# Laying dt and dt u in memory for one read per chunk, and placing the stages of four layers by their scans

## The chip, the cores and the metric

The kernel runs on one core of a Trainium2 chip. The metric is the time of the program on the device in microseconds; the runs before the change give 5587.08 us as the median of three (5577.02 to 5589.37). A separate, profiled execution took 5573.59 us, of which the profile's span is 5571.9 us. The text uses the profile's names of the engines: PE multiplies matrices (PEld loads its weights), DVE, ACT and POOL work element by element, and SP issues the transfers between memory and the on-chip buffer.

## The reference

Thirty-two sequences of 256 tokens with 256 features go through four layers, in fp32. Each adds its result to its input x:

- layer 0, a Mamba layer: normalize x, modulate, permute the tokens, scan, permute back, gate;
- layer 1, softmax attention with 16 heads, with a normalized and modulated output;
- layer 2, a Mamba layer without the permutation;
- layer 3, linear attention with 16 heads.

A Mamba layer projects the normalized input to a scan input and a gate of 512 channels each, runs a convolution of four taps and a SiLU over the first (this is u), and projects u to a step size dt per channel and to vectors B and C of 16 states per token. The core is

```
dA  = exp(dt_t[:, :, None] * A)                      # A is negative, 512 x 16
hst = hst * dA + (dt_t * u_t)[:, :, None] * B_t[:, None, :]
y   = einsum('bds,bs->bd', hst, C_t)                 # for t = 0 .. 255
```

followed by y + u D, a product with silu(z) and the output projection. The recurrence over 256 tokens runs for 512 x 16 = 8192 pairs of channel and state in each sequence and layer.

## The kernel before

**One scan.** `mamba_scan(L, b)` runs the recurrence of layer L (0 or 2) and sequence b in 16 steps k. A step handles one chunk of 128 channels (c = 0 to 3) and one group of four states (g = 0 to 3). The 128 partitions hold 32 channels (`CB`) for each of the four states of the group (`NG`), and the free dimension holds the four quarters of the chunk (`QB`) with 256 tokens each: 1024 elements. For that, dt and dt u of the chunk have to stand on the partitions four times, once for each state. A step consists of

- POOL: b = dt u times B (2.37 us each);
- ACT: h = exp(A dt), four operations of 256 columns;
- DVE: the scan h = h x + b over 1024 columns (2.29 us);
- the product with C: on DVE for even g (1.22 us), on POOL for odd g (2.36 us);
- PE: sums over the four states into y.

The tiles b lie in a ring of four buffers, h in two.

**What a scan needs first.** `mamba_ahead(L, b)` computes the scan's inputs: normalization, projection, convolution, u, B and C, dt (a softplus on ACT) and, on POOL, dtu = dt u. B and C go to memory and come back spread over partitions, eight fetches per scan. dt and dt u are written to memory (tiles `dtd` and `dtud`, 512 channels by 256 tokens, line 794), one transfer of 512 KB each. For each chunk, `mamba_scan` reads them back into `dtr` and `dtur`. As the state groups need four copies, and the quarters lie apart in memory, each tile takes four reads of 128 KB into 32 partitions each (line 839). `dtr` and `dtur` have two buffers each, so a chunk's reads wait until the chunk two before it has been used. All these transfers are issued on SP's queue, in order; a transfer that waits holds those behind it.

**Who sets the order.** The program isn't written in the order in which it runs. Each operation becomes a `Step` with an estimated cost and a due number, and `Plan.order` (line 255) replays the engines with these costs: at each time it takes, for an engine, the step with the earliest due number among those that could begin soonest. It also keeps track of buffers. The resulting order of each engine is fixed in the program, and the hardware then runs each engine's list in order. A fetch counts as 0.4 us of SP and 3 us until its data are there (`fetch`, `late`).

[...]the plan also tracks PE's work over windows. Where the work in the last window would fall under `NEED` = 1.1[...], and nothing else of weight is ready, `usual` (line 287) puts in a filler: a matmul with zeros into y, seen in the profile as y<-rows,zeros.

**Due numbers.** At the end of the function a loop over i from -1 to 34 places the stages in units of two: iteration i covers the due numbers 2i to 2i + 2. Layer 0's scan of sequence i stands in the first half. Layer 2's preparation for sequence i - 2 stands in the first half too, and its scan in the second. Layer 0's preparation for sequence i + 1 stands in the second half; attention of sequence i - 1 in 2i to 2i + 1.55; linear attention of sequence i - 3 from 2i + 1.55 to 2i + 2. So layer 2 follows two sequences behind layer 0. Below, a period is the pair of one first-layer scan (layer 0) and one second-layer scan (layer 2), a unit the time from the start of one scan to the start of the next.

Of the kernel before, what the change touches and what calls it, by code (L numbers as in the profile page):

```python
# [8 lines left out]
F32 = mybir.dt.float32  # L9
# [7 lines left out]
P = 128  # L17
S = 256
# [3 lines left out]
DI = 512  # L22
IC = DI // P
# [8 lines left out]
NG = 4  # L32
SG = NS // NG
CB = P // NG
QB = P // CB
# [28 lines left out]
}  # L64
NROWC = 512
MASK_ROW, MAX_ROW = DH, DH + 1


class Virtual:
# [72 lines left out]
class Step:  # L142


    def __init__(self, cost, due, then, area):
        self.cost, self.due, self.then, self.area = cost, due, then, area
        self.engine, self.calls, self.table = None, [], None
        self.before, self.after, self.new, self.uses = set(), [], [], set()
        self.parts, self.opens, self.closes = False, None, False


class Clock:
# [45 lines left out]
class Plan:  # L198
# [1 line left out]


    NEAR = 0.25
    NEED = 1.1
    IDLE = 0.47
    LATENCY = 0.15
    SWITCH = 1.3
# [30 lines left out]
    def use(self, s, view, written):  # L237
        t = view.tile
        keep = []
        for one in t.seen:  # L240
            o, lo, hi, w = one
            clash = o is not s and lo < view.hi and view.lo < hi and (w or written)
            if clash:
                s.before.add(o)
            if not (written and view.lo <= lo and hi <= view.hi and o is not s):
                keep.append(one)
        keep.append((s, view.lo, view.hi, written))
        t.seen = keep
        if t not in s.uses:
            s.uses.add(t)  # L250
            if not t.steps and t.real is None:
                s.new.append(t)
            t.steps.append(s)
# [169 lines left out]
def kernel(ctx: ExitStack, tc: tile.TileContext, t, out: bass.AP):  # L423
# [219 lines left out]
    def fetch(out, in_, late=3.0):  # L643
        at(0.4, then=late)
        nc.sync.dma_start(out=out, in_=in_)

    def mrow_of(b):

        m = mrow_bufs[mrow_at[0] % 2]
        mrow_at[0] += 1  # L650
        fetch(m[0:1, :], mterm[3][b : b + 1, :])
        return m
# [51 lines left out]
    def mamba_ahead(L, b, st):  # L704

        nm = f"{L}_{b}"
        x = x_of[b]
        gate = w2.tile([P, D], F32, name=f"gate_{nm}", tag="gate")
        fetch(gate, gate_d[L][b].partition_broadcast(P))

        xh = normed(x, nm)
        if L == 0:
            ps = mm(f"ga_{nm}")
            pv = ps.rearrange("p (c t) -> p c t", c=DC)
            for c in range(DC):
                at(0.96)
                for s in range(ST):
                    nc.tensor.matmul(pv[:, c, :], lhsT=xh[:, s, c * P : (c + 1) * P], rhs=onehot[:, s, :],
                                     start=(s == 0), stop=(s == ST - 1))
        else:  # L720
            pv = transposed(xh, nm)
        hT = w2.tile([P, DC, S], F32, name=f"hT_{nm}", tag="hT")
        evacuated(hT, pv, AF.Identity, lambda c: shift[L][:, c, b : b + 1], lambda c: gain[L][:, c, b : b + 1])

        yield 0.2

        wi = wt[f"L{L}_in"]
        xpad = w1.tile([P, IC, 3 + S], F32, name=f"xpad_{nm}", tag="tmp")
        at(0.3)
        nc.gpsimd.memset(xpad[:, :, 0:3], 0.0)  # L730
        sz = w2.tile([P, IC, S], F32, name=f"sz_{nm}", tag="sz")
        for m2 in range(IC):
            ps = mm(f"in_{nm}_{m2}")
            pv = ps.rearrange("p (c t) -> p c t", c=2)
            for j in range(2):
                m = 2 * m2 + j
                at(0.96)
                for k in range(DC):
                    nc.tensor.matmul(pv[:, j, :], lhsT=wi[:, k, m * P : (m + 1) * P], rhs=hT[:, k, :],
                                     start=(k == 0), stop=(k == DC - 1))  # L740
            at(0.49)
            if m2 < 2:
                nc.scalar.copy(xpad[:, 2 * m2 : 2 * m2 + 2, 3:], pv)
            else:
                nc.scalar.activation(sz[:, 2 * m2 - 4 : 2 * m2 - 2, :], pv, AF.Silu)
            yield 0.25 + 0.05 * m2

        u = w2.tile([P, IC, S], F32, name=f"u_{nm}", tag="u")
        for c2 in range(2):
            ps = mm(f"cv_{nm}_{c2}")  # L750
            for j in range(2):
                c = 2 * c2 + j
                at(1.83)
                for k in range(4):
                    nc.tensor.matmul(ps[:, j * S : (j + 1) * S], lhsT=taps[L][:, c, k, :],
                                     rhs=xpad[:, c, k : k + S], start=(k == 0), stop=(k == 3))
            at(0.8)
            for j in range(2):
                c = 2 * c2 + j
                nc.scalar.activation(u[:, c, :], ps[:, j * S : (j + 1) * S], AF.Silu, bias=col(f"L{L}_conv_b", c))  # L760
            yield 0.45 + 0.1 * c2


        ps = mm(f"xp_{nm}")
        R = DTR + 2 * NS
        at(1.9)
        for k in range(IC):
            nc.tensor.matmul(ps[:R, :S], lhsT=wt[f"L{L}_xp"][:, k, :], rhs=u[:, k, :],
                             start=(k == 0), stop=(k == IC - 1))
        xd = w2.tile([R, S], F32, name=f"xd_{nm}", tag="xd")  # L770
        at(0.28)
        nc.scalar.copy(xd, ps[:R, :S])
        bc_d = memory.tile([2 * NS, S], F32, name=f"bc_{nm}", tag="bc_d")
        fetch(bc_d, xd[DTR:R, :])

        yield 0.7


        dt = w1.tile([P, IC, S], F32, name=f"dt_{nm}", tag="tmp")
        dtu = w1.tile([P, IC, S], F32, name=f"dtu_{nm}", tag="dtu")  # L780
        for c2 in range(2):
            ps = mm(f"dt_{nm}_{c2}")
            at(1.06, area=512)
            for j in range(2):
                c = 2 * c2 + j
                nc.tensor.matmul(ps[:, j * S : (j + 1) * S], lhsT=wt[f"L{L}_dt"][:, 0, c * P : (c + 1) * P],
                                 rhs=xd[:DTR, :], start=True, stop=True)
            at(0.73)
            for j in range(2):
                c = 2 * c2 + j  # L790
                softplus(dt[:, c, :], ps[:, j * S : (j + 1) * S], col(f"L{L}_b_dt", c))
        yield 0.8

        dd = [memory.tile([DI, S], F32, name=f"{what}d_{nm}", tag=f"{what}d") for what in ("dt", "dtu")]
        at(2.4)
        nc.gpsimd.tensor_tensor(dtu, dt, u, ALU.mult)
        fetch(dd[1].rearrange("(c p) t -> p c t", p=P), dtu)
        at(0.3)
        nc.gpsimd.memset(dt[:, :, 0:1], NEVER)
        fetch(dd[0].rearrange("(c p) t -> p c t", p=P), dt)  # L800

        st[L, b] = (dd, u, sz, gate, bc_d)

# [10 lines left out]
    def mamba_scan(L, b, st):  # L814
# [16 lines left out]
        for k in range(IC * SG):  # L831
            yield k / steps
            c, g = divmod(k, SG)
            if g == 0:
                dr = []
                for i, what in enumerate(("dt", "dtu")):
                    dr.append(rep.tile(shape, F32, name=f"{what}r_{nm}_{c}", tag=what))
                    src = dd[i][c * P : (c + 1) * P, :].rearrange("(q d) t -> d q t", d=CB)
                    for n in range(NG):
                        fetch(dr[-1][n * CB : (n + 1) * CB], src)  # L840
            if c % 2 == 0 and g == 0:
                y = ybank.tile([P, 2, S], F32, name=f"y_{nm}_{c}", tag="y")
            b_ = ring.tile(shape, F32, name=f"b_{nm}_{k}", tag="b")
# [278 lines left out]
    def first_ahead(b, st):  # L1122
        x_of[b] = xp.tile([P, ST, D], F32, name=f"x_{b}", tag="x")
        fetch(x_of[b], t["x"][b].rearrange("(s p) d -> p s d", p=P))
        yield 0.05
        yield from mamba_ahead(0, b, st)

    def placed(gen, begin, end):

        place = begin  # L1130
        while True:
            yield place
            try:
                place = begin + (end - begin) * next(gen)
            except StopIteration:
                return
# [11 lines left out]

    x_of, ready = {}, {}
    for i in range(-1, B + 3):
        gens, i2 = [], 2.0 * i
        if 0 <= i < B:
            gens.append(placed(mamba_scan(0, i, ready), i2, i2 + 1.0))
        if 0 <= i - 2 < B:
            gens.append(placed(mamba_ahead(2, i - 2, ready), i2, i2 + 0.9))
            gens.append(placed(mamba_scan(2, i - 2, ready), i2 + 1.0, i2 + 2.0))
        if 0 <= i + 1 < B:
            gens.append(placed(first_ahead(i + 1, ready), i2 + 1.0, i2 + 1.9))  # L1160
        if 0 <= i - 1 < B:
            gens.append(placed(attention(i - 1), i2, i2 + 1.55))
        if 0 <= i - 3 < B:
            gens.append(placed(linear_attention(i - 3), i2 + (1.55 if i - 1 < B else 0.0), i2 + 2.0))
        interleave(gens)
    plan.carry_out()


# [90 lines left out]
```

## Time and profile before

| | |
|---|---|
| median of three runs | 5587.08 us |
| profiled execution, its own time | 5573.59 us |
| its span | 5571.9 us |
| granted PE clock, mean over the span | 0.958 |
| first b of the first scan | 119.64 us |
| first b of layer 2's scan of sequences 28, 29, 30, 31 | 5026.1, 5196.47, 5337.82, 5469.87 us |
| loads of ACT's function tables | 563 records, 1283 ns each |
| transfers on the hardware queue | 443.08 MB in 468480 packets, 30.3% of 16 engines' span |

The profile lists, for each group of instructions, the busy time, the mean duration of one, and the idle time of the engine just ahead of it with what ended it. A timeline lists single instructions with start and duration. A table of windows gives busy times in chosen stretches with the granted PE clock (1.00 is full, 0.50 half) and the mean busy share of the sixteen transfer engines. A matmul in fp32 has two records. The names are those of the tiles: b<-dtur,B is POOL's first product, h<-dtr,Aneg the exponential, b<-b,C POOL's product with C, s and ex the attention's scores and their exponentials.

### The profile page before, as it was taken

Reading aid. Unit: us, or ns where it says so; the run is one execution under the profiler, and the core shown is the slowest. Engines: PE = TensorE matmul, PEld = TensorE weight load, DVE = VectorE, ACT = ScalarE, POOL = GpSimd, SP = SyncE. Lnnn points to the kernel's source line nnn. Section 1 sums busy time; section 2 is a strip of 40 time slices with the busy share of each in tenths; the row PEclk is TensorE's granted clock in tenths of the full one; section 3 lists DMA queues with packets and bytes.
Section 4 is the critical chain, followed back from the end, with each engine's and each line's share of the span. In section 5 each row is a group of like instructions: output and inputs, shape, how many; then the busy total and the mean of one; then the engine's idle time right before and its main releaser. Section 6 shows DMA issues by size and latency. Waiting matters only on the chain.

```text
span 5571.9 us, 81780 instructions
## 1 busy us (share of the span) xinstructions
PE 5011.1 (90%) x29884; PEld 3375.8 (61%) x29884; DVE 4135.5 (74%) x4290; ACT 3638.7 (65%) x7325; POOL 3921.9 (70%) x2130
## 2 busy tenths in 40 slices
PE   6899898999999999999999999999999999998876
PEld 5566555566666566666566666566666566666554
DVE  2767787687777777777777787777787777777754
ACT  2567676676676666676666676676676676676543
POOL 1768777777777776777776677777677777677544
PEclk7999999999999999999999999999999999999988
DMA  4323223323223323323332323332323332323111
GB/s 141 84 58 93 78 77 91 84 70 87 81 75 92 85 78 78 88 69 92 85 78 77 89 70 95 81 84 76 84 73 91 86 87 72 87 77 79 50 48 50
DMA packets 468883, 448.30 MB, mean 80 GB/s; under 512 B 41600, under 2 KB 465120, under 8 KB 468480
## 3 DMA queue, kind: packets, MB, share of 16 engines
q1 hardware_dynamic: 468480, 443.08, 30.3%
q8 instruction: 235, 3.85, 0.3%
q14 instruction: 168, 1.38, 0.1%
HBM read 365.19 MB, written 77.73 MB: 79 GB/s over the span
## 4 chain that ended last, share of the span: by engine, by line
PE 21%; DVE 12%; POOL 10%; ACT 8%; DMA 6%; issue 4%; SPq 1%; POOLq 0%; ACTq 0%; DVEq 0%
POOL b L398 9%; ACT h L398 5%; PE cv L398 4%; DVE h L398 4%; PE y L398 4%; PE s L398 4%; DVE b L398 3%; PE in L398 3%; PE o L398 3%; DMA dtr<-dtd 2%; DMA dtd<-dt 2%; SPq L398 1%; ACT L398 1%; DVE st L398 1%; POOL dtu L398 1%
## 5 line engine op out<-in xcount | busy, mean ns | idle before, releaser
L398 POOL TENSOR_TENSOR b<-dtur,B 128x1024 f32<-128x1024 f32 x1024 | 2405.6, 2370 | 670.8 <-DMA dtur<-dtud 308.9
L398 ACT ACTIVATE h<-dtr,Aneg 128x256 f32<-128x256 f32 x4096 | 1699.0, 465 | 309.3 <-DVE b L398 182.5
L398 POOL TENSOR_TENSOR b<-b,C 128x1024 f32<-128x1024 f32 x512 | 1205.7, 2355 | 589.2 <-DVE b L398 564.0
L398 DVE TENSOR_TENSOR_SCAN h<-h,b 128x1024 f32<-128x1024 f32 x512 | 1173.0, 2291 | 510.4 <-ACT h L398 296.0
L398 DVE TENSOR_TENSOR_SCAN b<-h,b 128x1024 f32<-128x1024 f32 x512 | 1167.8, 2281 | 65.3 <-POOL b L398 34.8
L398 PE MATMUL y<-rows,zeros 128*128 128x256 f32 x3298 | 881.0, 399 | 0.0
L398 ACT ACT_TABLE_LOAD x563 | 722.3, 1283 | 171.4 <-DMA dtr<-dtd 116.0
L398 PE MATMUL y<-b,sel 128*32 128x256 f32 x8192 | 648.5, 395 | 176.8 <-POOL b L398 93.2
L398 PEld LDWEIGHTS y<-rows,zeros 128*128 128x128 f32 x3298 | 604.6, 195 | 193.9 <-issue 128.2
L398 DVE TENSOR_TENSOR b<-h,C 128x1024 f32<-128x1024 f32 x512 | 623.9, 1219 | 17.6 <-DVE h L398 0.5
L398 PE MATMUL in<-hT,w_L_in 128*128 128x256 f32 x2048 | 513.2, 390 | 14.8 <-DVE nm L398 5.0
L398 PE MATMUL cv<-xpad,taps 128*128 128x256 f32 x2048 | 499.1, 389 | 14.2 <-ACT xpad L398 9.2
L398 PEld LDWEIGHTS y<-b,sel 128*32 128x32 f32 x8192 | 177.8, 109 | 491.5 <-POOL b L398 181.1
L398 DVE TENSOR_REDUCE nm<-s 128x2 f32<-128x512 f32 x512 | 328.6, 683 | 178.2 <-PE s L398 176.3
L398 PEld LDWEIGHTS in<-hT,w_L_in 128*128 128x128 f32 x2048 | 370.8, 190 | 147.8 <-issue 36.8
L398 PEld LDWEIGHTS cv<-xpad,taps 128*128 128x128 f32 x2048 | 375.1, 190 | 125.3 <-issue 52.4
L398 ACT ACTIVATE ex<-s 128x512 f32<-128x512 f32 x512 | 276.2, 590 | 123.5 <-PE s L398 121.8
L398 PE MATMUL s<-q,k 32*128 32x256 f32 x2048 | 337.7, 412 | 18.2 <-ACT dt L398 12.2
L398 PE MATMUL s<-k,q 32*128 32x256 f32 x2048 | 300.0, 404 | 2.2 <-ACT sz L398 1.1
L398 PE MATMUL o<-w_L_out,u 128*128 128x256 f32 x1024 | 284.3, 433 | 7.7 <-ACT xpad L398 7.0
L398 ACT ACTIVATE xh<-x,nb,rs 128x256 f32<-128x256 f32 x256 | 138.6, 592 | 222.7 <-DVE nb L398 213.6
L398 PEld LDWEIGHTS s<-q,k 32*128 32x128 f32 x2048 | 200.6, 188 | 136.7 <-issue 75.3
(466 smaller groups left out, 5849.3 us busy)
## 6 DMA issues: line engine op xcount, KB each, us to landing
dtur<-dtud SPq DMA_DIRECT2D x1024, 128.0 KB
dtr<-dtd SPq DMA_DIRECT2D x1024, 128.0 KB
B<-bc SPq DMA_DIRECT2D x256, 128.0 KB
C<-bc SPq DMA_DIRECT2D x256, 128.0 KB
dtud<-dtu SPq DMA_DIRECT2D x64, 512.0 KB
dtd<-dt SPq DMA_DIRECT2D x64, 512.0 KB
x<-in_x SPq DMA_DIRECT2D x32, 256.0 KB
gate<-gate_d SPq DMA_DIRECT2D x64, 128.0 KB
```

The costliest lines, as they stand in the source:

```text
L398: made.append(getattr(engine, name)(*[real(a) for a in args], **{k: real(v) for k, v in kw.items()}))
```

## The change

1. *Layout.* `dtd` and `dtud` become tiles of shape [32, 4, 4, 256]: channel within a quarter, chunk, quarter, token. The four quarters of a chunk lie side by side in memory, 4 KB for each of 32 channels. A new function `by_channel` writes each of them in four transfers of 128 KB, one for each quarter, from 32 partitions each. The plan is told that the four don't clash (`group`, `aside`).
2. *Reads.* Each `dtr` and `dtur` tile takes one transfer of 512 KB into 128 partitions, whose source repeats the 32 channels four times. The plan counts 4 us for it.
3. *Places.* The due numbers now follow from a list of scans, with layer 2 one sequence behind layer 0 (`LAG` = 1): layer 0's scan of sequence 0, then of 1, layer 2's of 0, layer 0's of 2, layer 2's of 1, and so on, 64 scans without a gap. Every other stage is placed relative to the scans before and after it: attention of b begins with the end of layer 0's scan of b and takes 0.8 of the time to layer 2's preparation; that preparation starts 0.7 ahead of its scan and ends 0.2 ahead; linear attention begins after layer 2's scan and takes 1.2. All stages are interleaved at once and no longer by iteration.
4. *Fillers.* `NEED` becomes 1.05.

What each engine computes for the result stays the same.

```diff
-    NEED = 1.1
+    NEED = 1.05
...
-            clash = o is not s and lo < view.hi and view.lo < hi and (w or written)
+            aside = s.group is not None and o.group is s.group and w and written
+            clash = o is not s and lo < view.hi and view.lo < hi and (w or written) and not aside
...
+    def by_channel(d, src):
+        for q in range(QB):
+            at(0.4, then=3.0).group = d.tile
+            nc.sync.dma_start(out=d[:, :, q, :], in_=src[q * CB : (q + 1) * CB])
...
-        dd = [memory.tile([DI, S], F32, name=f"{what}d_{nm}", tag=f"{what}d") for what in ("dt", "dtu")]
+        dd = [memory.tile([CB, IC, QB, S], F32, name=f"{what}d_{nm}", tag=f"{what}d") for what in ("dt", "dtu")]
         at(2.4)
         nc.gpsimd.tensor_tensor(dtu, dt, u, ALU.mult)
-        fetch(dd[1].rearrange("(c p) t -> p c t", p=P), dtu)
+        by_channel(dd[1], dtu)
         at(0.3)
         nc.gpsimd.memset(dt[:, :, 0:1], NEVER)
-        fetch(dd[0].rearrange("(c p) t -> p c t", p=P), dt)
+        by_channel(dd[0], dt)
...
-                    dr.append(rep.tile(shape, F32, name=f"{what}r_{nm}_{c}", tag=what))
-                    src = dd[i][c * P : (c + 1) * P, :].rearrange("(q d) t -> d q t", d=CB)
-                    for n in range(NG):
-                        fetch(dr[-1][n * CB : (n + 1) * CB], src)
+                    dr.append(rep.tile([P, QB * S], F32, name=f"{what}r_{nm}_{c}", tag=what))
+                    fetch(dr[-1], dd[i][:, c, :, :].rearrange("d q t -> d (q t)").unsqueeze(0)
+                          .to_broadcast([NG, CB, QB * S]), late=4.0)
+                dr = [v.rearrange("p (q t) -> p q t", q=QB) for v in dr]
...
-    for i in range(-1, B + 3):
-        gens, i2 = [], 2.0 * i
-        if 0 <= i < B:
-            gens.append(placed(mamba_scan(0, i, ready), i2, i2 + 1.0))
...
+    scans = [(L, i - L // 2 * LAG) for i in range(B + LAG) for L in (0, 2) if 0 <= i - L // 2 * LAG < B]
+    place = {scan: n for n, scan in enumerate(scans)}
+    for b in range(B):
+        first, second = place[0, b], place[2, b]
+        gap = second - first - 1
+        gens.append(placed(first_ahead(b, ready), first - FIRST_AHEAD[0], first - FIRST_AHEAD[1]))
+        gens.append(placed(mamba_scan(0, b, ready), first, first + 1))
+        until = second - AHEAD[0] * min(1.0, gap / 2)
+        gens.append(placed(attention(b), first + 1, first + 1 + ATTN * (until - first - 1)))
+        gens.append(placed(mamba_ahead(2, b, ready), until, second - AHEAD[1] * min(1.0, gap / 2)))
+        gens.append(placed(mamba_scan(2, b, ready), second, second + 1))
+        gens.append(placed(linear_attention(b), second + 1, second + 1 + LINEAR))
+    interleave(gens)
```

with `LAG` = 1, `FIRST_AHEAD` = (1.4, 0.1), `AHEAD` = (0.7, 0.2), `ATTN` = 0.8 and `LINEAR` = 1.2.

More of the change, by code (lines that the diff above doesn't have):

```diff
@@ L66 @@
 MASK_ROW, MAX_ROW = DH, DH + 1
+LAG = 1
+FIRST_AHEAD = (1.4, 0.1)
+AHEAD = (0.7, 0.2)
+ATTN = 0.8
+LINEAR = 1.2
 class Virtual:
@@ L148, in __init__ @@
         self.before, self.after, self.new, self.uses = set(), [], [], set()
-        self.parts, self.opens, self.closes = False, None, False
+        self.parts, self.opens, self.closes, self.group = False, None, False, None
 class Clock:
@@ L241, in use @@
             o, lo, hi, w = one
-            clash = o is not s and lo < view.hi and view.lo < hi and (w or written)
+            aside = s.group is not None and o.group is s.group and w and written
+            clash = o is not s and lo < view.hi and view.lo < hi and (w or written) and not aside
             if clash:
                 s.before.add(o)
-            if not (written and view.lo <= lo and hi <= view.hi and o is not s):
+            if aside or not (written and view.lo <= lo and hi <= view.hi and o is not s):
                 keep.append(one)
@@ L1147, in interleave @@
                 live.remove(one)
-    x_of, ready = {}, {}
-    for i in range(-1, B + 3):
-        gens, i2 = [], 2.0 * i
-        if 0 <= i < B:
-            gens.append(placed(mamba_scan(0, i, ready), i2, i2 + 1.0))
[L1156 to L1165, printed above, removed]
+    x_of, ready, gens = {}, {}, []
+    scans = [(L, i - L // 2 * LAG) for i in range(B + LAG) for L in (0, 2) if 0 <= i - L // 2 * LAG < B]
[11 more added lines that the diff above has]
+    interleave(gens)
     plan.carry_out()
```

## The prediction

> **What bounds the kernel now.** I read the page first, for whether one engine is full.
>
> ```profile
> span 5571.9 us, 81780 instructions
> PE 5011.1 (90%) x29884; PEld 3375.8 (61%) x29884; DVE 4135.5 (74%) x4290; ACT 3638.7 (65%) x7325; POOL 3921.9 (70%) x2130
> L398 POOL TENSOR_TENSOR b<-dtur,B 128x1024 f32<-128x1024 f32 x1024 | 2405.6, 2370 | 670.8 <-DMA dtur<-dtud 308.9
> L398 PE MATMUL y<-rows,zeros 128*128 128x256 f32 x3298 | 881.0, 399 | 0.0
> ```
>
> PE looks full, but 881 us are filler matmuls (y<-rows,zeros). No engine is the bound over the whole span, so I cut it into stages by POOL's timeline: a scan starts with its first b. From 1440.62 to 5026.1 us the starts repeat every 164.7 us: 99 us for a first-layer scan, 66 for a second-layer scan. Busy times of these stages, then of the stretch from the first b to dtu, and of the stretch from dtu's end to the second scan's first b (columns: window, length, busy us of PE, PEld, DVE, ACT, POOL, granted clock, DMA share, GB/s):
>
> ```profile
> 1440.62:1539.62 99.00, 89.95 (x514) 63.01 (x513) 77.58 (x85) 62.73 (x123) 62.48 (x35) 0.97 0.28 75
> 1539.62:1605.31 65.69, 61.48 (x415) 39.25 (x414) 51.62 (x46) 51.14 (x106) 59.89 (x32) 1.00 0.36 94
> 1440.62:1518.62 78.00, 70.39 (x401) 49.84 (x399) 65.47 (x71) 52.79 (x107) 55.27 (x30) 0.96 0.17 49
> 1520.97:1539.62 18.65, 17.21 (x105) 11.49 (x104) 10.82 (x12) 7.61 (x12) 4.87 (x4) 1.00 0.76 182
> ```
>
> The second scan is POOL-bound (59.9 of 65.7). The first is not: POOL idles 22.7 us among the attention's PE and DVE work, then waits for the memory round trip of dt u. POOL's timeline at that place:
>
> ```profile
> 1518.62 2.35 POOL L398 TENSOR_TENSOR dtu<-dt,u 128x1024 f32<-128x1024 f32 x1
> 1529.46 2.35 POOL L398 TENSOR_TENSOR b<-b,C 128x1024 f32<-128x1024 f32 x1 [3.70 <-DVE b L398]
> 1539.62 9.31 POOL L398 TENSOR_TENSOR b<-dtur,B 128x1024 f32<-128x1024 f32 x4 [7.82 <-DMA dtur<-dtud]
> ```
>
> So a period is 78.0 + 2.35 + 18.65 + 65.7 = 164.7 us. PE worked 17.2 of the 18.65 us, mostly on real work, so this wait is only partly a loss today.
>
> How fast a transfer runs depends on its form. Around the first scan few things run, and four windows show one kind each: B and C broadcasts; the writes of dt and dt u; the broadcasts left over; the reads into dtr and dtur.
>
> ```profile
> 94.00:101.00 7.00, 5.78 (x25) 4.39 (x24) 0.00 (x0) 2.97 (x5) 2.45 (x2) 1.00 0.26 84
> 102.00:104.00 2.00, 0.00 (x0) 0.00 (x0) 0.00 (x0) 0.00 (x0) 0.00 (x0) 0.95 1.05 356
> 105.00:108.00 3.00, 0.00 (x0) 0.00 (x0) 0.00 (x0) 0.00 (x0) 0.00 (x0) 0.50 0.27 94
> 112.00:119.00 7.00, 7.00 (x30) 5.91 (x29) 0.00 (x0) 0.84 (x2) 0.00 (x0) 0.85 1.14 196
> ```
>
> The broadcasts never pass a share of about a quarter: four of sixteen engines, 94 GB/s. The present reads use all engines but get only 196 GB/s.
>
> [...]
>
> **The change, part by part.** Instruction orders are written out from both programs; durations are those of the rows.
>
> (1) *Reads.* Per chunk of 128 channels, eight reads of 128 KB become two of 512 KB. Their source is [4, 32, 1024] with a repeated first dimension, against 128 rows: B's form, hence four engines. Price of one: 5.6 us at 94 GB/s[...]. I take 5.2. Today a tile takes 2.7 us at 196 GB/s. If I am wrong and it spreads over sixteen, 1.4. In a steady period 16 tiles need 83 us and 16 B/C fetches of 128 KB 22 us of the same four engines, 105 of some 163: not the bound, but transfers queue up.
>
> (2) *Writes.* Two become eight, each reading 32 partitions: 5.5 us for both tiles at the reads' 196 GB/s instead of 3. A write landed 3.1 us after issue at 1521, and 8.4 us at 99.5, behind B and C. In the new order all eight B/C fetches stand directly ahead of it in SP's queue; I take 6.
>
> (3) *Round trip at the second scan.* dtur is read for two chunks, then dtr. From dtu's end: 6 + 5.2 + 2.6 for landing (the last scan's last read was issued at 5466.6 and its b began at 5469.9: 3.3 less 0.7 of transfer) = 13.8 us to the first b, and 6 + 3 x 5.2 + 2.6 = 24.2 to the first exponential (today 18.65 and about 19). POOL then has four b (9.4 us) before the ring of four buffers is full; the fifth needs exponential, scan, product and sum of the first, 1.7 + 2.3 + 1.2 + 0.6 after 24.2, so POOL waits 6.8 us more. On ACT's queue dt now stands behind the scan's last exponential, with xd's copy and a table load: 3 us ahead of dtu. Behind that exponential wait DVE's scans and PE's sums.
>
> (4) *Order of stages.* Attention moves mostly under the second scan. Per unit, counts times the rows' means: real PE work 86.0/54.1 becomes 79.2/60.8 us, DVE 69.4/47.3 becomes 62.7/54.0. Between first b and dtu POOL has 25 large operations instead of 22: 25 x 2.36 + 4 x 0.93 = 62.7 us; in the second unit 55.4. Its idle time amid other work is 22.7 + 5.8 = 28.5 us per period now; at best both units stand like the second one now, 12. With 7 us of PE and DVE work moved out of the full unit into the one with 35 fillers, I take 19.
>
> (5) *Fillers.* 50 per period become 41 (15/35 to 11/30), 0.53 us each (two records of 267 ns busy): 4.8 us of PE, of which the lower NEED explains part. Nothing separate is added: it lies within (4). In all 1649 become 1415.
>
> (6) *At nothing:* SP's issues fall from 2976 to 1824 at some 0.45 us; SP mostly waits for others, so nothing; were it the limit at the scan's start, fourteen fewer issues would gain 6 us there. Table loads 565 to 525 at 1.28 us lie under ACT's 35% idle; uncovered, 1.6 us per period.
>
> Sum of a steady period: 62.7 + 3 + 2.35 + 13.8 + 55.4 + 6.8 + 19 = 163 us.
>
> (7) *Ends.* Before: first b at 119.6, then 59 scans to 5026.1, then five scans in 546 us, because the last two sequences run through attention and the second layer's preparation uncovered (141 and 132 us, then 102). After: 120 + 74 for the first scan as now; the second lasts 145, because attention and preparation of sequence 0 stand uncovered behind it (10 us tail of the scan, 85 for attention, where the last one took 103 under a scan, 28 preparation from the 5417 to 5445 us of the last one, 15 round trip, rest normalizing); then 60 scans at half a period; scan 63 another 145 for the same reason; 103 for the last. 587 + 30 x 163 = 5477 us, 1.7 more outside the span (5573.6 against 5571.9), and the runs' median lies 13.5 above the profiled one: 5492 us, say 5490, 1.7% faster.
>
> **Rivals.**
> *Slower: the four-engine reads decide.* Place: the start of each second-layer scan. Break-even is a period of (5571.9 - 587) / 30 = 166.2 us, 3.2 more than my sum: first exponential at 27.5 instead of 24 us after dtu. For it: the queue on four engines at two thirds load, and a plan that allows 4 us for a read. Against: chunks later in a scan have some 14 us of POOL work as cover. With 6 us more per period, 169: 5670 us.
> *The reads spread over sixteen engines.* Round trip 10 and 13 us, no second wait: 62.7 + 3 + 2.35 + 10 + 55.4 + 19 = 152.5; 5177 us. Against: B's share of 0.27.
> *Only the ends change.* The better mix gives back just what the reads cost: 164.7, thus 587 + 4941 + 15 = 5543 us.
> *The clock.* NEED 1.05 leaves less margin[...]. The clock is 0.97 to 1.00 now.[...]
>
> **How the numbers follow.** Likeliest, a period of 155.5 to 165.5 (its own range 5270 to 5570, ends-only included): 0.50. Sixteen engines: 0.10. Within 0.2%, about what a measurement can tell, or 165.8 to 166.6: 0.05, the clock in it. Slower by the reads: 0.35. Faster 0.60, slower 0.35. The idle time in (4) reaches 28.5, a period of 172 and 5760 us; I leave out the last stretch and the lowest case: 5300 to 5710.
>
> **What would show it.** Right: a DMA share near 0.25 while dtur lands, first b about 14 and first exponential about 24 us after dtu, periods of 160 to 165 us, a gap of some 145 us before the third scan and the last. Wrong: dtur landing at a share near 1, or waits on dtr inside scans, or POOL still idle 28 us per period amid attention.

## The result and the profile after

The changed kernel takes 5947.48 us (median of four runs, 5935.32 to 5958.41) against 5582.05 us for the kernel before on the same chip: a ratio of 1.0653, with a 95% interval of 1.0624 to 1.0682. It is 6.5% slower, where 1.7% faster had been forecast. The page of its profile:

```profile
span 5938.0 us, 79158 instructions
...
PE 4985.7 (84%) x29416; PEld 3333.2 (56%) x29416; DVE 4093.0 (69%) x4290; ACT 3575.1 (60%) x7285; POOL 3928.3 (66%) x2130
...
L406 POOL TENSOR_TENSOR b<-dtur,B 128x1024 f32<-128x1024 f32 x1024 | 2403.6, 2361 | 1062.1 <-PE y L406 707.1
L406 ACT ACTIVATE h<-dtr,Aneg 128x256 f32<-128x256 f32 x4096 | 1700.9, 466 | 934.2 <-DMA dtr<-dtd 419.4
```

The busy times hardly moved (POOL 3921.9 before, PE 5011.1): the 366 us of longer span are waiting. POOL now waits for PE's sums, and ACT's exponentials wait 419.4 us for dtr, about 13 us once in each pair of scans (33.4 us in the trace of before; at a table load ahead of them ACT waits another 51.6 us for dtr, 116.0 before).

POOL's timeline gives the first b of every scan. "Unit" and "period" are those of the sections above, and every mean of units is over sequences 6 to 24. A first-layer unit takes 103.0 us (98.4 before) and a second-layer unit 74.5 (67.3). The second is the one that was POOL-bound. Here are one unit of each kind, then three stretches: the reads under way until the second scan's first b, from there to its first exponential, and the 10 us after it (columns as in the prediction: window, length, busy us of PE, PEld, DVE, ACT, POOL, granted clock, DMA share, GB/s):

```profile
1843.46:1945.72 102.26, 93.88 (x592) 63.86 (x593) 77.33 (x87) 67.59 (x137) 68.23 (x39) 1.00 0.21 70
1945.72:2020.27 74.55, 57.13 (x333) 37.34 (x332) 52.18 (x46) 45.38 (x93) 54.63 (x28) 0.89 0.26 88
...
1937.50:1945.70 8.20, 7.38 (x32) 5.70 (x33) 1.66 (x5) 4.66 (x6) 0.11 (x1) 1.00 0.24 79
1945.70:1956.10 10.40, 1.54 (x8) 1.01 (x6) 0.00 (x0) 0.00 (x0) 10.14 (x6) 0.71 0.28 110
1956.00:1966.00 10.00, 4.51 (x16) 3.07 (x17) 7.62 (x6) 9.85 (x19) 3.32 (x2) 0.50 0.31 121
```

In the second unit no engine is above 77% busy. In the fourth row (1945.70 to 1956.10) almost only POOL works: DVE and ACT stand still for 10 us, PE is busy for 1.5 us, and the transfer engines run at a share of 0.28. In the next row PE's granted clock is 0.50. The POOL timeline at that place:

```profile
1924.18 2.37 POOL L406 TENSOR_TENSOR dtu<-dt,u 128x1024 f32<-128x1024 f32 x1 [3.22 <-ACT dt L406]
...
1938.19 0.11 POOL L406 MEMSET xpad<- 128x12 f32 x1 [6.30 <-DMA dtd<-dt]
1945.72 6.94 POOL L406 TENSOR_TENSOR b<-dtur,B 128x1024 f32<-128x1024 f32 x3 [7.43 <-DMA dtur<-dtud]
...
1962.68 2.35 POOL L406 TENSOR_TENSOR b<-dtur,B 128x1024 f32<-128x1024 f32 x1 [6.73 <-PE y L406]
```

dtu ends at 1926.55; the first b starts 19.2 us later, and the fifth b waits 6.7 us for a free buffer of the ring. ACT's timeline, and SP's in between:

```profile
1956.10 3.26 ACT L406 ACTIVATE h<-dtr,Aneg 128x256 f32<-128x256 f32 x8 [13.05 <-DMA dtr<-dtd]
```

```profile
1924.43 0.61 SPq L406 DMA_DIRECT2D C<-bc  x1
1925.09 1.81 SPq L406 DMA_DIRECT2D B<-bc  x1
1926.95 1.30 SPq L406 DMA_DIRECT2D C<-bc  x1
1928.35 3.36 SPq L406 DMA_DIRECT2D dtud<-dtu  x4
1931.82 4.30 SPq L406 DMA_DIRECT2D dtd<-dt  x4
1936.85 1.12 SPq L406 DMA_DIRECT2D dtur<-dtud  x2
1938.14 3.78 SPq L406 DMA_DIRECT2D dtr<-dtd  x2
```

The first exponential comes 29.6 us after dtu. SP issued the first read only at 1936.85, 10.3 us after dtu. The view of what SP waited for from 1936 to 1937.2 us (total, times, longest) has the landing of dt u's write in it:

```profile
SPq L406 <- DMA dtud<-dtu: 0.6, 2, 0.3
```

The trace also holds the times at which the engines of a transfer report their completion, and these tell what the landing came with. The eight B/C fetches issued just ahead of the writes, with four reports each, landed one after another, some 1.5 us apart, until 1935.6 us. Of the sixteen reports of the first write twelve came at 1931.4 to 1931.6, the other four only at 1935.5 to 1935.9; the last of dt u's four writes landed at 1936.8. Issuing became slow as well (1.8 and 1.3 us for the last two B/C fetches instead of 0.5 to 0.6), but SP was done with the eight writes at 1936.12, before the data had landed. Of the 4.3 us in the row of dt's four writes about 2 us are waits for B/C fetches; a single issue took 0.55 us. It is the same in the mean of sequences 6 to 24: last B/C fetch landed 8.6 us after dtu, last write issued at 9.2, dt u landed at 9.9, first read issued at 10.0. By the same reports, four for each read, the read tiles land one after another, dtur at 1945.6 and 1951.0, dtr at 1956.1 and 1961.2: the first dtr tile 10.4 us after the first b.

The run in four parts. "To layer 2's first scan" is that scan's first b; the period is the mean of the 30 that follow; then the last two stretches. The last four rows are kernels of the next section.

| kernel | to layer 2's first scan | 30 periods of | last but one to last scan | last scan to end | span |
|---|---|---|---|---|---|
| before | 382.5 | 165.2 | 132.1 | 102.0 | 5571.9 |
| predicted | 339 | 163 | 145 | 103 | 5477 |
| after | 358.4 | 177.1 | 154.8 | 111.7 | 5938.0 |
| layout alone | 414.9 | 191.0 | 140.2 | 111.2 | 6396.7 |
| placement and NEED, old transfers | 343.1 | 170.6 | 132.1 | 101.1 | 5694.7 |
| after, reads in four | 327.2 | 171.5 | 134.0 | 102.4 | 5707.7 |
| the same, xpad apart | 337.9 | 164.1 | 132.4 | 103.7 | 5496.3 |

### The profile page after: what moved, and what is told of

The parts are those of the page before. It is cut to its first block, busy times and chain, and to the rows that moved or that the text cites. A ratio compares the mean times of both kernels' runs of the same rounds, so it can differ in the third digit from the quotient of the medians.

```text
span 5938.0 us, 79158 instructions
## 1 busy us (share of the span) xinstructions
PE 4985.7 (84%) x29416; PEld 3333.2 (56%) x29416; DVE 4093.0 (69%) x4290; ACT 3575.1 (60%) x7285; POOL 3928.3 (66%) x2130
## 5 line engine op out<-in xcount | busy, mean ns | idle before, releaser
L406 ACT ACTIVATE h<-dtr,Aneg 128x256 f32<-128x256 f32 x4096 | 1700.9, 466 | 934.2 <-DMA dtr<-dtd 419.4
L406 PE MATMUL y<-rows,zeros 128*128 128x256 f32 x2830 | 767.9, 406 | 0.0
L406 ACT ACT_TABLE_LOAD x523 | 671.0, 1283 | 110.9 <-DMA dtr<-dtd 51.6
L406 PEld LDWEIGHTS y<-rows,zeros 128*128 128x128 f32 x2830 | 521.5, 197 | 195.1 <-issue 139.1
L406 PE MATMUL cv<-xpad,taps 128*128 128x256 f32 x2048 | 508.6, 405 | 18.8 <-ACT xpad L406 9.3
L406 PE MATMUL in<-hT,w_L_in 128*128 128x256 f32 x2048 | 496.1, 391 | 23.8 <-ACT xpad L406 20.3
L406 PEld LDWEIGHTS cv<-xpad,taps 128*128 128x128 f32 x2048 | 418.4, 207 | 100.5 <-ACT sz L406 23.0
L406 PEld LDWEIGHTS in<-hT,w_L_in 128*128 128x128 f32 x2048 | 384.4, 195 | 109.3 <-issue 26.1
L406 PE MATMUL s<-k,q 32*128 32x256 f32 x2048 | 328.3, 416 | 10.1 <-DMA k<-mterm 9.5
L406 PE MATMUL s<-q,k 32*128 32x256 f32 x2048 | 315.7, 407 | 24.6 <-DVE y L406 24.6
L406 ACT COPY xpad<-in 128x512 f32<-128x512 f32 x128 | 71.8, 586 | 372.5 <-POOL xpad L406 317.1
L406 POOL TENSOR_TENSOR dtu<-dt,u 128x1024 f32<-128x1024 f32 x64 | 150.7, 2355 | 180.9 <-ACT dt L406 180.9
L406 PEld LDWEIGHTS s<-k,q 32*128 32x128 f32 x2048 | 198.7, 192 | 114.0 <-issue 62.8
```

Source lines behind the costliest of these rows:

```text
L406: made.append(getattr(engine, name)(*[real(a) for a in args], **{k: real(v) for k, v in kw.items()}))
```

## The experiments

Ratios are to the kernel before on the same chip, 5575 to 5582 us, with 95% intervals.

### One half of the change each

The first kernel is before with the new tiles `dtd` and `dtud`, `by_channel` and the single reads; the second is after with those parts as they were:

```diff
 # e1, on the kernel before
+dd = [memory.tile([CB, IC, QB, S], ...)]; by_channel(dd[1], dtu); by_channel(dd[0], dt)
+fetch(dr[-1], dd[i][:, c, :, :]...to_broadcast([NG, CB, QB * S]), late=4.0)
 # e2, on the kernel after: the same lines back to before.py's
```

> The kernel before with the new layout, writes and reads alone; the old placement and NEED 1.1 stay. Theory T (transfers: the four-engine reads, about 5.2 us a tile instead of 2.7, and the eight small writes behind B and C are what cost the 12.4 us per period): slower than before by most of the loss, a period near 175 us, 5800 to 5950 us. Theory P (placement: attention and the second layer's preparation stand where nothing covers the round trip or dt, and POOL idles amid them): within 50 us of before, 5530 to 5640 us.

> The changed kernel with the old layout, writes and reads; the new placement and NEED 1.05 stay. Theory T: the loss is gone, a period of 160 to 165 us, 5450 to 5600 us. Theory P: as slow as the changed kernel, a period of 174 to 178 us, 5850 to 5950 us. If the two need each other, neither this nor the layout alone shows the loss.

The layout alone takes 6400.79 us, 1.1478 (1.1454 to 1.1503); the placement alone, NEED included, 5721.63 us, 1.0255 (1.0221 to 1.0289). Neither theory had this. Both halves lose, and they don't add: under the old placement the layout costs 826 us, under the new one 226. The waits of ACT on dtr differ in the same way. The first line is of the layout alone, the second of the changed kernel (engine, line, waited for: us in total, times, longest):

```profile
ACT h L399 <- DMA dtr<-dtd: 990.1, 63, 30.8
```

```profile
ACT h L406 <- DMA dtr<-dtd: 419.4, 32, 22.8
```

With the old placement ACT waits at the start of nearly every scan, 63 of 64, with the new one only at 32, 29 of them of the second layer. In the new placement POOL works 14.2 of the 16.9 us between the first layer's dtu and its first b, in the layout alone 5.5 of 15.5: the first layer's round trip is covered. The second layer's dtu stands at the very end of the scan before, with little behind it.

### The form of the reads

The same bytes, layout and rows of 4 KB, but one transfer for each of the four copies, with 32 as the leading dimension on both sides, where the single read's source has 4. On after (e3) and on the layout alone (e5):

```diff
-fetch(dr[-1], dd[i][:, c, :, :].rearrange("d q t -> d (q t)").unsqueeze(0)
-      .to_broadcast([NG, CB, QB * S]), late=4.0)
+for n in range(NG):
+    fetch(dr[-1][n * CB : (n + 1) * CB], dd[i][:, c, :, :].rearrange("d q t -> d (q t)"), late=4.0)
```

> The changed kernel with each tile's one read of 512 KB split into four of 128 KB, one for each copy, 32 rows of 4 KB against 32 partitions, so that a transfer can use sixteen engines. Theory T: two tiles of dtur and the first of dtr land in 5 to 8 us instead of 19, the first exponential comes 15 to 20 us after dtu instead of 29.6, a period of 165 to 168 us, 5570 to 5680 us. Theory P: the same landing times but POOL's idle time moves elsewhere, 5850 us or more.

> The kernel before, old placement, with the new layout and writes, but each tile read in four transfers of 32 rows of 4 KB, one per copy. Theory R (of the new layout only the form of the one read costs time; the layout and the eight small writes are harmless): the 826 us that the whole layout cost in the old placement vanish, 5540 to 5640 us. Theory W (the small writes and the longer rows have a part in it): 5700 us or more.

e3 takes 5711.05 us, 1.0238 (1.0211 to 1.0266), 31 us above the range of theory T: 236 us less than after and as much as the old transfers under the same placement (5722). e5 takes 5750.52 us, 1.0307 (1.0291 to 1.0322): 650 of the layout's 826 us vanish, but it stands in theory W's range. The table of windows at the reads, of the layout alone and then of e3:

```profile
112.00:122.00 10.00, 8.26 (x31) 6.63 (x29) 0.00 (x0) 0.65 (x1) 3.92 (x2) 0.83 0.26 95
```

```profile
2542.00:2546.00 4.00, 4.00 (x20) 3.54 (x19) 1.46 (x4) 1.48 (x3) 0.00 (x0) 1.00 0.84 198
```

Share 0.26 and 95 GB/s become 0.84 and 198 GB/s. The reports of completion of the other two kernels point the same way: in after the single read has four of them, in before each read of 128 KB into 32 partitions sixteen, at a share of 1.14 (112 to 119 us), and a B/C fetch, whose source has a leading dimension of 4, four, at 0.27 (105 to 108 us). So in these runs the forms with 4 in front ran on four engines, those with 32 on all sixteen. ACT's wait at the exponentials shrinks from 419.4 us in 32 waits to this line of e3:

```profile
ACT h L406 <- DMA dtr<-dtd: 7.3, 3, 3.2
```

In e5 it shrinks from 990.1 to 76.7 us.

The tiles land even faster than expected: from the issue of the first read to the first dtr tile it takes 4.7 us on average, 19.7 in after. But the scan doesn't start earlier, as I had expected of e3. The first b comes later after dtu (23.4 us on average, 19.1 in after), and the first exponential 28.8 us after dtu (29.7 in after), not 15 to 20. In the scan at 2551 us it comes 25.7 us after dtu, behind other work of ACT; dtr had landed 15 us before. What differs is what the engines do meanwhile. In after ACT's list has the exponentials next: they wait for dtr, POOL fills the ring and stops, and PE is busy for 1.5 of 10.4 us and then has a granted clock of 0.50. In e3 ACT and PE go on; from the first b at 2551.65 to the first exponential at 2557.50, and in the 10 us after it:

```profile
2551.65:2557.50 5.85, 5.85 (x28) 5.13 (x28) 0.00 (x0) 3.04 (x7) 5.85 (x3) 1.00 0.29 84
2557.50:2567.50 10.00, 9.34 (x49) 7.53 (x48) 8.16 (x5) 8.83 (x22) 7.31 (x4) 1.00 0.05 15
```

In the second unit POOL's waits on PE's sums fall from 16.7 to 6.2 us, and the unit from 74.5 to 66.4; 4.2 us of that only because the unit is counted from a later first b. From the end of dtu to the end of the unit it is 93.7 us in after and 89.8 in e3, from the first unit's start to dtu 81.5 and 78.7. A period falls by 6.7 us, to 170.8 and not to 165 to 168, the stretches at the ends by 61 us in all, and the mean clock of the span rises from 0.919 to 0.948. The plan of e3 has other transfers and so another order, and e3 was run in one order only.

### The plan told of the real latency

e4 is after with 9 us for a write and 10 for a read in the plan (3 and 4 before); only the order changes.

> The changed kernel, the plan alone told of longer transfers: 9 us for a write (3 before) and 10 us for a read (4 before). Theory T in the form that the plan doesn't know the latency: PE, ACT and DVE get other work ahead of the first exponential of the second scan, the wait of ACT on dtr falls from 13 to under 6 us per period, 5700 to 5850 us. Theory P, or T in the form that the wait itself is the loss: within 60 us of the changed kernel, 5880 to 6000 us.

5820.58 us, 1.0433 (1.0406 to 1.0459), in the first range: 127 us less than after. The waits of ACT on dtr fall from 419.4 to 245.3 us in 34 waits, 7.2 each, less than expected. The first exponential still comes 29.7 us after dtu on average, as in after; what changed is the order of the work around it. That the gain comes from the plan's knowing the latency is not shown: the same kind of edit costs 363 us in e12 below.

### The buffer that dt shares with xpad

The placement with the old transfers (e2) shows another stop, at the end of each first-layer scan. Lines from ACT's, PE's and DVE's timelines of e2, then POOL's:

```profile
2544.39 1.07 ACT L406 COPY xpad<-in 128x512 f32<-128x512 f32 x2 [11.25 <-DMA dtd<-dt]
2545.03 6.00 PE L406 MATMUL o<-w_L_out,u 128*128 128x256 f32 x16 [5.58 <-ACT xpad L406]
2551.08 0.69 DVE L406 TENSOR_TENSOR yg<-o,gate 128x512 f32<-128x512 f32 x1 [11.88 <-PE o L406]
```

```profile
2555.89 0.22 POOL L406 TENSOR_SCALAR va<-mv 128x2 f32<-128x2 f32 x1 [11.43 <-DVE mv L406]
2558.91 9.29 POOL L406 TENSOR_TENSOR b<-dtur,B 128x1024 f32<-128x1024 f32 x4 [2.02 <-DMA dtur<-dtud]
```

xpad of the next preparation uses the buffer of dt (tag "tmp", one buffer), so it waits until dt has been written to memory. ACT stands 11 us on it. PE's results wait in PSUM to be copied; the scan's output product o comes 5.6 us late; yg, x and the statistics mv follow; and POOL, whose list has the normalization of the scanned sequence ahead of the second scan's first b, waits 11.4 us for mv. dtur itself is late by only 2 us more. In after ACT stands at the same place, 12.1 us at 1926, as POOL may not clear the edge of xpad before dt has landed. The edit gives xpad its own buffer, paid with one of four buffers for the small statistics:

```diff
-xpad = w1.tile([P, IC, 3 + S], F32, name=f"xpad_{nm}", tag="tmp")
+xpad = w1.tile([P, IC, 3 + S], F32, name=f"xpad_{nm}", tag="xpad")
-space("small", 4)
+space("small", 3)
```

> The changed kernel with the reads in four, and xpad in a buffer of its own instead of sharing dt's (3 instead of 4 buffers for the small statistics pay for the space). Theory X (the placement loses because the next preparation's xpad waits for dt's write to memory at the end of each first-layer scan, and ACT and PE stand behind it): the waits of ACT and POOL on dtd vanish, a period falls from 171 to 160 to 165 us, 5390 to 5550 us. Theory C (the chain from attention through the second layer's preparation is too short of slack in itself): the wait moves to another step, 5650 to 5730 us.

> The changed kernel, reads unchanged, with xpad in a buffer of its own (3 buffers for the small statistics). Theory X, with the two losses adding: 5947 less 6 to 11 us per period, 5620 to 5770 us. If the reads' landing ends the wait in any case: 5880 to 5960 us.

> The kernel before with xpad in a buffer of its own (3 buffers for the small statistics). Theory X says that the old placement leaves little on this wait (7 us per period of ACT and POOL together, most of it under other work): 5480 to 5580 us. If the buffer is worth as much here as in the new placement: below 5450 us.

> The changed kernel with the old layout, writes and reads, and xpad in a buffer of its own (3 buffers for the small statistics). If the new layout with reads in four is neither better nor worse than the old one under the new placement, this stands within 40 us of that kernel: 5460 to 5545 us. If the single writes help once the buffer is apart: 5380 to 5460 us.

| kernel | without | xpad apart | ratio to before |
|---|---|---|---|
| e6: after, reads in four | 5711 | 5502.75 | 0.9861 (0.9847 to 0.9876) |
| e10: placement, old transfers | 5722 | 5573.35 | 0.9995 (0.9984 to 1.0005) |
| e8: before | 5579 | 5548.84 | 0.9943 (0.9928 to 0.9958) |
| e7: after | 5947 | 5995.79 | 1.0744 (1.0726 to 1.0762) |

With fast transfers and the new placement the buffer is worth 208 and 148 us, in the old placement 30 (in the range of theory X). With the four-engine reads it is worth nothing: e7 is 48 us slower than after, 36 us worse than even the second range. That dtr's landing ends the wait there in any case fits, but isn't shown. The waits at xpad in e3:

```profile
POOL xpad L406 <- DMA dtd<-dt: 254.6, 42, 12.8
ACT xpad L406 <- POOL xpad L406: 212.6, 21, 12.1
ACT xpad L406 <- DMA dtd<-dt: 111.5, 10, 15.4
```

In e6 those on dt's write are gone; ACT waits for the projection itself, POOL for the convolution that reads the xpad before:

```profile
ACT xpad L406 <- PE in L406: 149.8, 102, 4.4
POOL xpad L406 <- PE cv L406: 149.2, 32, 18.6
```

The units are shorter, 97.8 and 65.6 us, and e6 stands in the range of theory X, 5390 to 5550 us. But POOL's wait on mv has not fallen with the buffer: it is 333.0 us in e3 and 377.8 in e6. So the first links of the chain, ACT and POOL at xpad behind dt's write, are what the buffer ended; the last one, POOL behind mv, is not. e10 landed 28 us above the range of "neither better nor worse". The smaller buffer for statistics was not tried alone.

### The small writes

> The kernel before with its two writes of 512 KB split into four of 128 KB each, from 32 partitions, in the old layout; reads and placement are those of before. Theory W (the 171 us that the new layout still cost in the old placement with the reads in four come from the small writes): 5680 to 5760 us. Theory S (they come from the longer rows and the order of the issues, not from the writes): 5560 to 5620 us.

The kernel before with `fetch(dd..., dtu)` replaced by four transfers of 32 partitions each, in the old layout, and the same for dt: 5663.6 us, 1.0159 (1.0142 to 1.0176). 87 us, between the two ranges: about half of what e5 still lost. Whether the writes do it can't be told from the order they bring about, as the next runs show.

### How much the planned order scatters

> The kernel before with one number of its plan changed by 0.01 us, the cost of issuing a transfer, 0.41 instead of 0.40: no operation is added, removed or changed, only the replay breaks ties in another way. If the planned order scatters little: within 15 us of before. If differences of 70 to 90 us, as NEED and the split writes gave, can come from the order alone: 40 us or more away from before, in either direction.

> As the last one, but 0.39 instead of 0.40. The same two expectations: within 15 us of before if the planned order scatters little, 40 us or more away, in either direction, if it scatters by as much as NEED and the split writes moved it.

> The changed kernel with reads in four and xpad apart (5503 us), the plan's cost of issuing a transfer 0.41 instead of 0.40. If its gain is that of the mended buffer and reads: within 30 us, 5470 to 5535 us, still faster than before. If it was a lucky order: over 5550 us.

> The changed kernel with reads in four and xpad apart (5503 us), the plan alone told of 9 us for a write instead of 3. If what is left of POOL's waits at the start of the second scan comes from a plan that believes in early landings: 5380 to 5460 us. If the plan's order matters little once the buffer and the reads are mended: 5470 to 5540 us.

```diff
 def fetch(out, in_, late=3.0):
-    at(0.4, then=late)
+    at(0.41, then=late)      # e13, e16; 0.39 in e14
```

Before with 0.41: 1.0045 (1.0031 to 1.0059); with 0.39: 1.0035 (1.0022 to 1.0048), 22 to 24 us slower, between the two ranges, though no operation differs. The mended kernel e6 with 0.41: 5582.79 us, 1.0009 (0.9998 to 1.002), 80 us slower than e6 and in the range of a lucky order. And e6 with 9 us for a write in the plan (e12, expected to gain): 5865.4 us, 1.0513 (1.0492 to 1.0534), 363 us slower, outside both of its ranges; POOL's waits on mv rise from 377.8 to 440.8 us, and DVE's on PE's v from 50.6 to 352.0. An order found by replaying costs is thus a draw, with a spread of 0.4% in one kernel and 1.5% in the other, and what a single order shows below some 80 us is no verdict on the edit. The reads (236 and 650 us) and the buffer (208, or 128 with e16's order, and 148) stand above it; e9's 87 us do not by much. As e12 shows, a change of the plan that does more than break ties can move the time by far more; every edit here changes the plan too, so the sizes are less sure than the waits that went with them.

### NEED

> The kernel before with NEED 1.05 instead of 1.1, nothing else. As in the prediction, fewer fillers (1374 instead of 1649) gain nothing by themselves: 5560 to 5610 us. If the lower margin costs half-clock windows[...]: 5650 us or more, at a mean clock under 0.95.

> The changed kernel with the old layout, writes and reads, and with NEED 1.1 again: the placement alone. If NEED costs 69 us here as in the old placement: 5640 to 5670 us against 5722 with NEED 1.05, and the placement's own loss is about 80 us. If the loss is the placement's (dt's buffer): 5700 to 5740 us.

> The changed kernel with reads in four, xpad apart and NEED 1.1 instead of 1.05. If NEED costs some 65 us wherever it stands: 5430 to 5520 us against 5503 and 5583 of the two orders with NEED 1.05, at a clock above 0.956. If its two differences so far were scatter: anywhere from 5480 to 5600 us.

> The changed kernel with NEED 1.1 instead of 1.05 and nothing else. If NEED costs some 65 us wherever it stands: 5860 to 5900 us against 5947, a mean clock above 0.92. If the four-engine reads hide it, since PE stands idle at the scan's start whatever fillers are planned later: 5920 to 5970 us.

| kernel | NEED 1.1 | NEED 1.05 |
|---|---|---|
| before (e11) | 5577 | 5645.92, 1.0124 (1.0108 to 1.014) |
| placement, old transfers (e15) | 5658.6, 1.0139 (1.012 to 1.0157) | 5722 |
| after, reads in four, xpad apart (e17) | 5536.97, 0.9914 (0.9898 to 0.993) | 5503 and 5583 (e6, e16) |
| after (e18) | 5959.16, 1.0677 (1.066 to 1.0695) | 5947 |

The lower value lost 69 and 63 us in two pairs and nothing in the other two. By the expectations, e11 stands 4 us short of its second range, e15 in the range of "NEED costs 69 us", e17 in that of scatter alone, and e18 in that of the reads hiding it. In e11 PE does 109 us less filler work, and still ends later, at a mean clock of 0.946 against 0.958. That fits the thought that fewer fillers cost clock, but with a scatter of 22 to 80 us and two pairs on each side it stays open. That PE's clock depends on its work, on which NEED and the fillers rest, was the author's assumption. After has stretches that fit it: from 1950.10 to 1967.17 us PE was busy for 5.7 of 17.1 us, and the granted clock was 0.50; from 1967.20 to 1974.00 it was busy throughout, and the clock was 1.00.

## Why the prediction was wrong

The forecast was 5490 us and a range of 5300 to 5710. The rival "slower: the four-engine reads decide" came nearest. It put the reads at 6 us more per period, and with the reads in four 6.7 us per period came back (177.5 to 170.8); but 14.5 us more than the forecast 163 were measured. One reading of the trace of before was off too: 164.7 us is the length of one period; from 1539.62 to 5026.1 us the second-layer scans start 166.0 us apart on average.

*(1) Reads: right.* Four engines, as the likeness to the B fetches had suggested (four reports, share 0.24 to 0.28), and 79 to 110 GB/s. The 5.2 us a tile were the author's estimate, somewhat under the 5.6 of 94 GB/s; the tiles landed one after another, 5.4, 5.1 and 5.1 us apart, and the first dtr tile came 10.4 us after the first b, as two tiles had been priced. Queueing within a scan was not the loss: after the scan's start ACT waits for dtr no more.

*(2) Writes: mis-sized.* Priced at 6 us from dtu to landing; it was 10.2 us in the scan shown: 1.8 until the first write was issued and 8.4 until the last had landed, the very 8.4 us that the prediction quotes from 99.5 us in the trace of before. The place was right (all eight B/C fetches directly ahead), but a value between the two examples was taken, though four of the first write's sixteen reports came only at 1935.5 to 1935.9 us, with the end of those fetches at 1935.6. In (6) I had priced SP's issues at 0.45 us and said that their number costs nothing. Single issues took up to 1.8 us here, but the first read waited for the landing and not for SP, so that this cost anything isn't shown.

*(3) Round trip: mis-sized by 5.3 us.* From dtu to the first b 13.8 had been expected and 19.1 were measured, to the first exponential 24.2 and 29.7; some 4 us of that are those of (2). The distance of 10.4 us between the two was right, and so was the ring: 6.7 us of waiting for the fifth b against 6.8 in the scan shown. With a first exponential at 29.7 us the prediction's own break-even (27.5) had been passed; only the terms of (2) kept the sum below it.

*(4) Order of stages: the step that failed.* Its counts were right: POOL works 62.7 us before dtu (62.7 expected) and 55.0 in the second unit (55.4). Its idle time was not. I took 3 us for dt, 6.8 for the ring and 19 amid other work, 28.8 together; measured are 18.8 before dtu and 19.5 in the second unit, 38.3. I assumed that a lighter first unit would fill up and that the second would stay as tight as the second unit of before. But the second unit begins with 10.4 us in which DVE and ACT do nothing and PE works 1.5, and for the next 10 PE's granted clock is 0.50; POOL then waits 16.7 us per unit for PE's sums, of which only 6.8 had been counted; with the reads in four it is 6.2. Nothing in its sum priced what stands still behind a late dtr apart from the ring. Without the 3 and the 6.8 us, 28.5 us are left of the 38.3, not 19: as much as before, and the amount that the prediction named as a sign of being wrong, though 9.9 of it stand at PE's sums in the second unit and not amid attention.

The same step failed for a second reason, which the reads hide: the placement with the old transfers loses 5.4 us per period, NEED included (5722 us, and 5659 with NEED 1.1). Its idle time amid other work fell from 28.8 to 25.4 us only (17.9 before dtu, 7.5 in the second unit), not to 19, and the stretch from dtu to the first b grew from 18.2 to 26.3. xpad behind dt's write stood in the orders of the engines; I named dt behind the scan's last exponential and did not price who waits for dt's buffer.

*(5) Fillers at nothing: open.* See NEED. What a smaller margin costs in half clock was not shown.

*(7) Ends: right apart from the reads.* 587 us had been expected of the three stretches outside the 30 periods; after has 624.9, with reads in four 563.6, and before 616.6. With fast reads the saving is there, 23 us larger than forecast; with the four-engine reads these stretches take 61 us more, and it is gone.

Sum of a period: 163 expected; 5.3 more for the round trip and 9.5 more idle time give 177.8, against 177.5 measured over the same sequences. Of the 365 us of loss, the form of the reads accounts for 236 (shown by e3). For the rest, the xpad buffer is shown as a cause by two pairs (e3 with e6 and e16, e2 with e10), but only once the reads are fast; its 30 us in the old placement are hardly more than an order scatters. What is left after both are mended is a kernel at 5503 us in one order and 5583 in another: the best found is 1.4% faster than before, by the table 43 us of it at the ends and 33 us in the periods, and how much of that is the placement and how much the luck of the order is not settled. That its period of 164.1 us is near the forecast 163 is luck: the first b comes 21.0 us after dtu and not 13.8, and other terms are smaller.

## What to carry to other kernels

Merging transfers saves issues (2048 reads became 512 here), but look at how many engines the merged form uses: one read of 512 KB with a leading dimension of 4 ran at a share of 0.26 and 95 GB/s (e1), four of 128 KB with 32 at 0.84 and 198 GB/s (e3). Before moving a stage to the end of another, ask of every tile that it writes who gets the buffer next and what that engine holds up meanwhile. Where a program computes the order, run it a few times with costs that differ by nothing before believing a per cent.

## What the runs showed that was not expected

- Writes close behind B/C fetches landed only with the last four of their sixteen reports. Of the first dt u write in after, issued at 1928.35, twelve came after 3.1 to 3.3 us, the last four at 7.2 to 7.5 us, with the end of the B/C fetches (four reports each, the last at 1935.6). In before the write issued at 99.50 has twelve reports at 103.1 to 103.3 and four at 107.4 to 107.9, the last B/C fetch landed at 106.6. Where the last fetch issued ahead of it had landed at 1521.5, the write issued at 1520.99 had all sixteen by 1523.95.
- Issues on SP's queue took 0.5 to 0.6 us each for the first six B/C fetches of after (1921.43 to 1924.43 us); then 1.81 and 1.30 for the last two, with those before them under way until 1932.6, 3.8 for the two dtr reads, and 5.25 for the gate's fetch of 128 KB at 1941.97, behind these reads. SP issued nothing else in that time, as if it waited.
- Rows of 4 KB gained little bandwidth over rows of 1 KB: 198 GB/s with 32 partitions a transfer (e3) against 196 before; on four engines 87 GB/s (1940 to 1945 us in after) to 102 (1951 to 1955) against 94. Both figures of the sixteen-engine form are little more than half of the 356 GB/s at which before wrote from 128 partitions (102 to 104 us); what limits them isn't shown.
- A change of 0.01 us in a plan's cost moved the kernel before by 0.4% and the mended one by 1.5%.
